# Router logits and gate scores with the weights as the loaded operand, in four column quarters of TensorE

## The chip, the cores and the metric

The kernel runs on one core of one Trainium2 chip. TensorE (PE in the profile; PEld is its weight load) multiplies, VectorE (DVE) does element-wise work and reductions, ScalarE (ACT) does copies and exponentials, GpSimd (POOL) does the rest of the element-wise work and issues the indexed transfers, and SyncE (SP) issues the ordinary transfers. The metric is the device time of one execution in microseconds (us), the median of several runs. Everything is float32; one float32 matmul of the program shows in the profile as two weight loads and two matmuls.

## The reference

Two decoder layers on x of 8 x 256 x 512 (2048 tokens of width 512). Two places matter here. The first is the feed-forward of layer 0, a mixture of 8 experts of which each token takes two:

```python
logits = h @ router_w.T                       # (2048, 512) @ (512, 8)
probs = jax.nn.softmax(logits, axis=-1)
vals, idx = lax.top_k(probs, 2)
```

The second is the feed-forward of layer 1, an attention in which each token picks one of 16 heads for its key and value:

```python
gating = jax.nn.softmax(x @ W_gate.T, axis=-1)   # (2048, 512) @ (512, 16)
idx = jnp.argmax(gating, axis=-1)
k_shared = one_hot(idx) . k ;  v_shared = one_hot(idx) * gating . v
```

Between and around them stand a differential attention, a long convolution, a causal self attention and a cross attention, each with a residual and a layer norm.

## The kernel before

Tokens come in 16 tiles of 128. The stages run one after another: `diff_attention`, `long_conv`, the expert blocks (`blocks`), `self_attention`, `cross_attention` and `routed_attention`.

**The router** (`router`, `route`, `token_tile`, `choose`, `send`, `table`). It runs in two halves of eight token tiles. The first half stands inside `long_conv` after head 15 of 32; there the order of instructions on each engine is made by the framework's scheduler when the program is built, so that convolution work (`ps_y` on TensorE, `z`, `yc`, `kv` on VectorE) stands between the router's. The second half stands in `blocks`, inside a section whose order on TensorE, VectorE and ScalarE is the order of the program text: blocks 0 to 2 of the experts (`gate_up`, and `turn`, which transposes the next block), with three or two token tiles after each, then `choose`. One `token_tile` transposes the tile to token-major form (`pt_c`, L731), copies it out by ScalarE (L737), takes mean and variance (L145, L146), norms the tile before it (L722), and computes the logits: four k-steps, each with 128 tokens as the loaded operand and 8 columns of router weights as the streamed one (`ps_r`, through `project`, L172), copied to `raw` by ScalarE (L744). `choose` turns `raw` into the two chosen experts by some thirty small VectorE operations; `send` computes each token's slot and scatters the rows by 16 indexed transfers on GpSimd (L789). The PSUM tag `tr` has two buffers, which `pt_c`, `ps_r` and `turn` share.

**The gates** (`gates` in `routed_attention`). The stage works in four groups of 512 tokens. `turned_group` transposes four token tiles (`pt`, L195) and ScalarE copies each of them into a quarter of `xT` (L196). `gates` then makes, for each of the four token tiles, four k-steps with 128 tokens loaded and 16 columns streamed (`ps_g`), and VectorE does the softmax and the maximum. `feature_block` (queries, `ps_f`), `token_block` (keys and values, `ps_t`), and `keys_turned` (`pt_k`) follow. A planner in `causal_attention` doses these pieces between the attention units: each piece has a cost (`MM` = 0.86, `TR` = 0.45 us, the gates 0.8), a slot by which it must be done, and a place in a queue; `fill` takes pieces from it up to a budget for each slot, `need` takes what is due. The order of the engines here is that of the program text too. The PSUM tag `mm` has three buffers. In attention units, `products` (L1264, L1274) uses TensorE in four column quarters: for each of four heads 32 loaded columns and up to 256 streamed ones, into 32 partitions of PSUM each.

`routed_weights` loads the weights of this stage before the cross attention begins.

Of the kernel before, what the change touches and what calls it, by code (L numbers as in the profile page):

```python
# [17 lines left out]
F32 = mybir.dt.float32  # L18
BF16 = mybir.dt.bfloat16
AF = mybir.ActivationFunctionType  # L20
ALU = mybir.AluOpType
# [29 lines left out]
def decoder_kernel(ctx: ExitStack, tc: tile.TileContext, a: dict, out: bass.AP):  # L51
# [117 lines left out]
    def project(ps, lhsT, rhs, n=KB):  # L169

        for k in range(n):
            nc.tensor.matmul(ps, lhsT=lhsT(k), rhs=rhs(k), start=(k == 0), stop=(k == n - 1))  # L172

    MM, TR = 0.86, 0.45

# [314 lines left out]
    def long_conv(router, load_experts, xh, ch, ps_t, meanwhile):  # L490
# [5 lines left out]
        with ExitStack() as st:  # L496
# [18 lines left out]
            for h in range(NH):  # L515
                i, at = divmod(h * NHEAD, P)
                hs = slice(at, at + NHEAD)
                xv, cv = xh[i], ch[i]
                wt = work.tile([P, D], F32, tag="wt", name="wt", bufs=3)
                nc.sync.dma_start(out=wt, in_=toeplitz(h))  # L520
                if h == 2:
                    load_experts()

                kv = work.tile([P, KB, B, NHEAD, NHEAD], F32, tag="kv", name="kv")
                for k in range(KB):
                    (nc.gpsimd if k == KB - 1 else nc.vector).tensor_tensor(  # L526
                        kv[:, k],
                        xv[:, k, :, hs].unsqueeze(2).broadcast_to(shape),
                        cv[:, k, :, hs].unsqueeze(3).broadcast_to(shape),
                        ALU.mult,  # L530
                    )
# [12 lines left out]
                nc.gpsimd.tensor_tensor(  # L544
                    r,
                    cv[:, :, :, hs],
                    us.unsqueeze(3).broadcast_to([P, KB, B, NHEAD]),
                    ALU.mult,
                )
                nc.gpsimd.tensor_tensor(r, r, xv[:, :, :, hs], ALU.add)  # L550
                yc = work.tile([P, KB, B, NHEAD], F32, tag="yc", name="yc")
                for lb in range(KB):
                    ps = psum.tile([P, B, NHEAD, NHEAD], F32, tag="y", name="ps_y")
                    project(
                        ps,
                        lambda k: wt[:, (lb - k) * P : (lb - k + 1) * P],
                        lambda k: kv[:, k],
                        n=lb + 1,
                    )
                    z = work.tile([P, B, NHEAD, NHEAD], F32, tag="z", name="z", bufs=3)  # L560
                    nc.vector.tensor_tensor(
                        z, ps, cv[:, lb, :, hs].unsqueeze(2).broadcast_to(shape), ALU.mult
                    )
                    nc.vector.tensor_reduce(yc[:, lb], z, AX.X, ALU.add)  # L564
                nc.gpsimd.tensor_tensor(xv[:, :, :, hs], r, yc, ALU.add)  # L565
                if h < 2:
                    for t in range(h * PH + 1, (h + 1) * PH, 2):
                        turn(t)
                    if h == 1:
                        x_first.close()  # L570
                if h == NH // 2 - 1:
                    tiles, choose, send, table = route(ps_t, xv, i)
                    for f in (*tiles, choose, send, table, meanwhile):
                        f()
            return route(ps_t, xh[1], 1)

# [42 lines left out]
    def experts(rt):  # L619
# [26 lines left out]
                    ].rearrange("e p c -> p e c"),  # L646
                )

        rw = rt.tile([P, KB, E], F32, tag="rw", name="rw")
        idx = index_row(rt, E, "idx_e")  # L650
        before = rt.tile([P, P], F32, tag="before", name="before")
        ones = rt.tile([P, P], F32, tag="ones_m", name="ones_m")
# [23 lines left out]
        def router(work, rows_late):  # L676
            nc.sync.dma_start(
                out=rw, in_=a["L0_ffn_router_w"].rearrange("(k p) e -> p k e", p=P)
            )

            nc.gpsimd.memset(ones, 1.0)
            nc.gpsimd.affine_select(
                out=before,
# [17 lines left out]
            def route(ps_t, xv, half):  # L701
# [22 lines left out]
                    )  # L724
                    nc.sync.dma_start(out=xd[tiles[i]], in_=r)

                def token_tile(i):
                    b = tiles[i] // 2
                    pt = ps_t.tile([P, KB, P], F32, tag="tr", name="pt_c")
                    for k in range(KB):  # L730
                        nc.tensor.transpose(pt[:, k, :], xv[:, k, b, :], ident)  # L731
# [7 lines left out]
                    rsqrt(rstd[:, i : i + 1], mv[:, i, 1:2], 1.0)  # L739
                    if i:  # L740
                        norm(i - 1)
                    pr = ps_t.tile([P, E], F32, tag="tr", name="ps_r")
                    project(pr, lambda k: xv[:, k, b, :], lambda k: rw[:, k, :])
                    nc.scalar.copy(raw[:, i, :], pr)  # L744

                def choose():
                    norm(PH - 1)

                    lg = rt.tile(shape, F32, tag="lg", name="lg", bufs=2)
# [61 lines left out]
                    for v in (v1, v2):  # L811
                        nc.vector.tensor_tensor(v, v, vs, ALU.mult)

                return [lambda i=i: token_tile(i) for i in range(PH)], choose, send, table

            return route

# [91 lines left out]
        def blocks(ps_t, buffers, late_tokens, meanwhile):  # L909


            with ExitStack() as st:
# [102 lines left out]
                with tc.manual_schedule(  # L1015
# [6 lines left out]
                    turn(0)  # L1022
                    for b in range(3):
                        if b:
                            tiles[3 * b - 1]()
                        gate_up(b)
                        load(b + 4)
                        for f in tiles[3 * b : 3 * b + 2]:
                            f()
                        turn(b + 1)  # L1030
                    choose()
                    gate_up(3)
# [643 lines left out]


    def routed_weights(w):
        return load_w(w, 0, a["L1_ffn_W_qkv"], 3 * D), load_w(
            w, 3 * D * KB, a["L1_ffn_W_gate"], H1  # L1680
        )

    def routed_attention(wqkv, wg):

# [2 lines left out]
        def prepare(work, pools, g, at, here):  # L1687
# [6 lines left out]
            ind = work.tile([P, TPG, H1], F32, tag="ind", name="ind")  # L1694
            itop = work.tile([P, TPG, H1], F32, tag="itop", name="itop")

            def gates():
                ps = pools.tile([P, TPG, H1], F32, tag="mm", name="ps_g")
                for ti in range(TPG):
                    project(  # L1700
                        ps[:, ti, :],
                        lambda k: xT[0][:, k, ti * P : (ti + 1) * P],
                        lambda k: wg[:, k, :],
                    )
                gate = work.tile([P, TPG, H1], F32, tag="gate", name="gate")
                nc.vector.tensor_copy(gate, ps)
                softmax_small(work, gate, H1)
                top = work.tile([P, TPG], F32, tag="top", name="top")
                first_max(work, gate, H1, idx, top, ind)
# [26 lines left out]
                nc.scalar.copy(kT, pt.rearrange("p t q -> p (t q)"))  # L1736

            xT, need = turned_group(work, pools, g)
            need.append((0, [(0.8, gates)]))
            need.append((0, feature_block(pools, qT, xT, wqkv, 0, 0, HD1**-0.5)))  # L1740
            for ti in range(TPG):
                need.append(
                    (0, token_block(pools, xT, wqkv, D, ti, lambda ps, ti=ti: key(ti, ps)))
                )
            for c in range(1, 3):
                need.append((0, feature_block(pools, qT, xT, wqkv, 0, c, HD1**-0.5)))
            need.append((0, [(TR, keys_turned)]))
            for c in range(3, KB):
                need.append((c, feature_block(pools, qT, xT, wqkv, 0, c, HD1**-0.5)))
# [146 lines left out]
```

## Time and profile before

| what | value |
|---|---|
| median of three runs | 2196.74 us (2194.0 to 2199.11) |
| the profiled execution, its time | 2205.52 us |
| its span from first to last instruction | 2203.7 us |
| TensorE busy | 2054.0 us, 93% of the span |
| VectorE busy | 1275.9 us, 58% |
| GpSimd busy | 826.9 us, 38% |
| ScalarE busy | 605.1 us, 27% |
| mean granted TensorE clock | 0.971 |

The profiled execution is a single one: its own time is 1.8 us over its span, and 8.8 us over the median of the timed runs. Durations in the rows below are of this execution. A timeline row gives the start in us, the duration, the engine, the line, the operation with output and inputs, the shapes and the count, and in brackets how long the engine was idle before and who ended that. The duration of a merged matmul row is from the first start to a modelled end; the distance to the next row's start is the time that TensorE spent on it.

### The profile page before, as it was taken

How to read it: one execution, taken by the hardware profiler on the slowest of the kernel's cores; microseconds unless marked ns; L12 is line 12 of the kernel's file. 1: busy time of each engine (PE TensorE's matmuls, PEld its weight loads, DVE VectorE, ACT ScalarE, POOL GpSimd, SP SyncE). 2: the span in 40 equal slices, each digit the busy share in tenths (PEclk: the TensorE clock that was granted, in tenths of full speed). 3: DMA queues.
4: the chain of work that ended last, by engine and by line, in shares of the span. 5: the costliest groups of instructions: out<-in, count | busy, mean ns of one | idle time of the engine just before them, and what ended most of it. 6: DMA issues, size and time to landing. Idle time of an engine off the chain costs nothing. (4 is left out here: it accounts for less than half of the span.)

```text
span 2203.7 us, 36445 instructions
## 1 busy us (share of the span) xinstructions
PE 2054.0 (93%) x15296; PEld 1264.8 (57%) x15296; DVE 1275.9 (58%) x1923; ACT 605.1 (27%) x773; POOL 826.9 (38%) x918
## 2 busy tenths in 40 slices
PE   8989999889999998999968999999999999999995
PEld 6646655544453464555545665656877875545543
DVE  4677777658888962222235756556344343576777
ACT  4545555410010021111113333330110110333342
POOL 2667777646557622000034544333000000142343
PEclk9989999989999999999979999999999999999998
DMA  6899802235133153131141201002100100000000
GB/s 220 331 384 381 311 1 69 78 93 186 34 115 120 29 172 121 60 144 63 43 144 30 77 20 58 2 1 96 36 22 20 39 0 1 1 11 11 11 18 32
DMA packets 110035, 197.61 MB, mean 90 GB/s; under 512 B 7088, under 2 KB 30768, under 8 KB 109872
## 3 DMA queue, kind: packets, MB, share of 16 engines
q1 hardware_dynamic: 104752, 178.49, 23.3%
q0 software_dynamic: 5120, 16.78, 2.2%
q8 instruction: 123, 2.02, 0.4%
q14 instruction: 40, 0.33, 0.0%
HBM read 93.54 MB, written 112.20 MB: 93 GB/s over the span
## 5 line engine op out<-in xcount | busy, mean ns | idle before, releaser
L1282 DVE RECIPROCAL rsum<-ps_pv 128x256 f32<-128x256 f32 x128 | 224.5, 1754 | 243.7 <-PE ps_pv L1274 243.4
L172 PE MATMUL ps_y<-kv,wt 128*128 128x512 f32 x640 | 281.1, 597 | 4.5 <-POOL kv L526 3.8
L1238 ACT ACTIVATE pT<-ps_k 128x1536 f32<-128x1536 f32 x128 | 185.8, 1451 | 286.0 <-PE ps_k L1230 282.1
L1178 DVE TENSOR_REDUCE neg<-rows 128x12 f32<-128x1536 f32 x128 | 223.0, 1742 | 54.1 <-POOL rows L1169 54.0
L1169 POOL TENSOR_SCALAR_AFFINE_SELECT rows<-rows 128x1024 f32<-128x1024 f32 x128 | 141.5, 1105 | 246.8 <-ACT rows L1167 246.5
L1167 ACT COPY rows<-ps_q 128x1536 f32<-128x1536 f32 x128 | 184.3, 1440 | 179.4 <-PE ps_q L1158 130.2
L1239 POOL TENSOR_SCALAR_AFFINE_SELECT pT<-pT 128x1024 f32<-128x1024 f32 x128 | 141.1, 1103 | 242.6 <-ACT pT L1238 242.4
L172 PEld LDWEIGHTS ps_y<-kv,wt 128*128 128x128 f32 x640 | 120.3, 191 | 153.6 <-issue 135.2
L1249 POOL TENSOR_TENSOR pT<-pT 128x512 f32<-128x512 f32 x112 | 145.7, 1301 | 9.3
L183 PE MATMUL ps_f<-xT,w_l1a 128*128 128x256 f32 x512 | 129.2, 400 | 12.2 <-ACT xT L196 12.2
L1084 POOL DMA_INDIRECT w_l1x<-ys,slots x32 | 32.7, 1023 | 279.8 <-DMA ys<-y_m 272.1
L183 PE MATMUL ps_t<-w_l1f,xT 128*128 128x512 f32 x256 | 121.9, 611 | 0.0
L183 PEld LDWEIGHTS ps_f<-xT,w_l1a 128*128 128x128 f32 x512 | 96.9, 197 | 33.8 <-ACT xT L196 14.3
L999 PE MATMUL po_m<-dn,hT 128*128 (+1 forms) x216 | 104.4, 621 | 12.0 <-ACT hT L992 10.5
L140 POOL TENSOR_SCALAR rstd<-bn_mv 128x1 f32<-128x1 f32 x80 | 16.6, 207 | 216.2 <-DVE bn_mv L146 208.1
L1274 PE MATMUL ps_pv<-pT,ones_v 128*32 128x256 f32 (+1 forms) x1152 | 84.7, 376 | 7.2 <-POOL pT L1249 7.0
L564 DVE TENSOR_REDUCE yc<-z 128x64 f32<-128x512 f32 x128 | 86.1, 674 | 6.2 <-POOL w_l1a L565 5.7
L981 DVE TENSOR_TENSOR h_b<-h_b,pg 128x352 f32<-128x352 f32 x36 | 18.8, 521 | 101.3 <-ACT h_b L980 101.3
L1158 PE MATMUL ps_q<-kz,qT 32*128 32x128 f32 x1536 | 62.2, 292 | 15.2 <-ACT pT L1238 13.3
L1158 PEld LDWEIGHTS ps_q<-kT,qT 32*128 32x128 f32 x1536 | 49.2, 188 | 44.4 <-issue 21.2
L1158 PEld LDWEIGHTS ps_q<-kz,qT 32*128 32x128 f32 x1536 | 49.8, 190 | 41.0 <-ACT pT L1238 26.2
L183 PE MATMUL ps_f<-xT,w_l 128*128 128x256 f32 x256 | 71.2, 406 | 0.9 <-POOL w_l L273 0.7
(326 smaller groups left out, 3768.7 us busy)
## 6 DMA issues: line engine op xcount, KB each, us to landing
xs<-zero SPq DMA_DIRECT2D x8, 4352.0 KB
ys<-zero SPq DMA_DIRECT2D x8, 4352.0 KB
filters<-in_L_xattn_k SPq DMA_DIRECT2D x4, 2560.0 KB
first_h<-xs SPq DMA_DIRECT2D x36, 256.0 KB
ys<-y_m SPq DMA_DIRECT2D x36, 256.0 KB
gu<-in_L_ffn_gate_up_proj SPq DMA_DIRECT2D x3, 2816.0 KB
wt<-filters SPq DMA_DIRECT2D x32, 256.0 KB
x<-in_x SPq DMA_DIRECT2D x16, 256.0 KB
```

The costliest lines, as they stand in the source:

```text
L172: nc.tensor.matmul(ps, lhsT=lhsT(k), rhs=rhs(k), start=(k == 0), stop=(k == n - 1))
L183: nc.tensor.matmul(ps[0], lhsT=lhsT(k), rhs=rhs(k), start=(k == 0), stop=(k == KB - 1))
L564: nc.vector.tensor_reduce(yc[:, lb], z, AX.X, ALU.add)
L999: nc.tensor.matmul(po, lhsT=hT[:m, i, :], rhs=dn[i][:m, bass.ds(e, 1), :], start=(i == 0), stop=(i == len(FCH) - 1),)
L1158: nc.tensor.matmul(block[:, s, j, :], lhsT=q(rows, c, b * S + i * P, P), rhs=k(rows, c, b * S + keys * P, P), start=True, stop=True,)
L1167: nc.scalar.copy(d.rearrange("p j s k -> p s j k"), block)
L1169: nc.gpsimd.affine_select(out=rows, in_=rows, compare_op=ALU.is_ge, fill=-FAR, base=0, pattern=[[0, 8], [-1, P]], channel_multiplier=1,)
L1178: return lambda: nc.vector.tensor_reduce(neg[u // upb % 2][:, :, :, c], d, AX.X, ALU.max, negate=True)
L1238: nc.scalar.activation(p[:, 0:3].rearrange("p j s q -> p s j q"), block, AF.Exp)
L1239: nc.gpsimd.affine_select(out=p[:, 0:2].rearrange("p j s q -> p (j s) q"), in_=p[:, 0:2].rearrange("p j s q -> p (j s) q"), compare_op=ALU ...
L1249: nc.gpsimd.tensor_tensor(p[:, 3], p[:, 1], p[:, 2], ALU.add)
L1282: nc.vector.reciprocal(r, ps[:, 1, :])
```

## The change

Two new helpers are used in both places. `columns_by_block` takes 512 tokens at once: each of the four k-steps has its weight columns as the loaded operand, 32 columns wide, in a column quarter of TensorE of its own, and the 512 tokens as the streamed one. The results stand in 32 partitions of one PSUM tile each, unsummed, and one ScalarE copy of 128 x 512 takes them out. `sum_of_blocks` then transposes the four 128 x 128 pieces of that copy and sums the four k-steps with one VectorE reduction. Since 32 columns are loaded where 8 or 16 are meant, the weight tiles get a zeroed tail (a GpSimd memset for the router, a VectorE memset for the gates), and the columns beyond are not read.

In the router, `token_tile` no longer computes logits: after the fourth and the eighth tile of a half, `columns_by_block` is called, and `logits` (the transposes and the sum) at the beginning of the next tile or of `choose`. In the routed attention, `gates` is split into `gate_parts` and `gates`, with a feature block between them, and the second feature block is moved ahead of the key blocks. The gate weights are loaded ahead of `W_qkv`.

```diff
+    def columns_by_block(ps, dst, w, n, rhs):
+        for k in range(KB):
+            nc.tensor.matmul(
+                ps[32 * k : 32 * k + 32, :],
+                lhsT=w[:, n * k : n * k + 32],
+                rhs=rhs(k),
+                start=True,
+                stop=True,
+            )
+        nc.scalar.copy(dst, ps)
+
+    def sum_of_blocks(dst, pt, parts):
+        for i in range(pt.shape[1]):
+            nc.tensor.transpose(pt[:, i, :], parts[:, i * P : (i + 1) * P], ident)
+        n = dst.shape[2]
+        nc.vector.tensor_reduce(
+            dst, pt.rearrange("p t (k r n) -> p t r n k", k=KB, n=n)[:, :, 0], AX.X, ALU.add
+        )
...
+            nc.gpsimd.memset(rows_w[:, KB * E :], 0.0)
...
+                def logits():
+                    pt = ps_t.tile([P, PH // 2, P], F32, tag="tr", name="pt_r")
+                    i, rows = part.pop()
+                    sum_of_blocks(raw[:, i : i + PH // 2, :], pt, rows)
+
-                def token_tile(i):
+                def token_tile(i, pool):
                     b = tiles[i] // 2
+                    if i == PH // 2:
+                        logits()
...
-                    pr = ps_t.tile([P, E], F32, tag="tr", name="ps_r")
-                    project(pr, lambda k: xv[:, k, b, :], lambda k: rw[:, k, :])
-                    nc.scalar.copy(raw[:, i, :], pr)
+                    if (i + 1) % (PH // 2) == 0:
+                        j = i + 1 - PH // 2
+                        rows = pool.tile([P, D], F32, tag="rpart", name="rpart", bufs=1)
+                        columns_by_block(
+                            ps_t.tile([P, D], F32, tag="tr", name="ps_r"),
+                            rows,
+                            rows_w,
+                            E,
+                            lambda k: xv[:, k, j : i + 1, :],
+                        )
+                        part.append((j, rows))
 
                 def choose():
+                    logits()
                     norm(PH - 1)
...
     def routed_weights(w):
-        return load_w(w, 0, a["L1_ffn_W_qkv"], 3 * D), load_w(
-            w, 3 * D * KB, a["L1_ffn_W_gate"], H1
-        )
+        g = 3 * D * KB
+        load_w(w, g, a["L1_ffn_W_gate"], H1)
+        nc.vector.memset(w[:, g + KB * H1 : g + KB * H1 + 32 - H1], 0.0)
+        return load_w(w, 0, a["L1_ffn_W_qkv"], 3 * D), w[:, g:]
...
+            def gate_parts():
+                columns_by_block(
+                    pools.tile([P, GT], F32, tag="mm", name="ps_g"), part, wg, H1, lambda k: xT[0][:, k, :]
+                )
+
             def gates():
-                ps = pools.tile([P, TPG, H1], F32, tag="mm", name="ps_g")
-                for ti in range(TPG):
-                    project(
-                        ps[:, ti, :],
-                        lambda k: xT[0][:, k, ti * P : (ti + 1) * P],
-                        lambda k: wg[:, k, :],
-                    )
+                pt = pools.tile([P, TPG, P], F32, tag="mm", name="pt_g")
                 gate = work.tile([P, TPG, H1], F32, tag="gate", name="gate")
-                nc.vector.tensor_copy(gate, ps)
+                sum_of_blocks(gate, pt, part)
...
-            need.append((0, [(0.8, gates)]))
+            need.append((0, [(MM, gate_parts)]))
             need.append((0, feature_block(pools, qT, xT, wqkv, 0, 0, HD1**-0.5)))
+            need.append((0, [(TR, gates)]))
+            need.append((0, feature_block(pools, qT, xT, wqkv, 0, 1, HD1**-0.5)))
             for ti in range(TPG):
...
-            for c in range(1, 3):
-                need.append((0, feature_block(pools, qT, xT, wqkv, 0, c, HD1**-0.5)))
+            need.append((0, feature_block(pools, qT, xT, wqkv, 0, 2, HD1**-0.5)))
```

More of the change, by code (lines that the diff above doesn't have):

```diff
@@ L572, in long_conv @@
                     tiles, choose, send, table = route(ps_t, xv, i)
-                    for f in (*tiles, choose, send, table, meanwhile):
+                    for f in tiles:
+                        f(work)
+                    for f in (choose, send, table, meanwhile):
                         f()
@@ L647, in load_gu_last @@
                 )
-        rw = rt.tile([P, KB, E], F32, tag="rw", name="rw")
+        rows_w = rt.tile([P, KB * E + 32 - E], F32, tag="rw", name="rw")
+        rw = rows_w[:, : KB * E].rearrange("p (k e) -> p k e", k=KB)
         idx = index_row(rt, E, "idx_e")
@@ L725, in norm @@
                     nc.sync.dma_start(out=xd[tiles[i]], in_=r)
-                def token_tile(i):
+                part = []
+                def logits():
[3 more added lines that the diff above has]
+                def token_tile(i, pool):
                     b = tiles[i] // 2
+                    if i == PH // 2:
+                        logits()
                     pt = ps_t.tile([P, KB, P], F32, tag="tr", name="pt_c")
@@ L812, in table @@
                         nc.vector.tensor_tensor(v, v, vs, ALU.mult)
-                return [lambda i=i: token_tile(i) for i in range(PH)], choose, send, table
+                return [lambda pool, i=i: token_tile(i, pool) for i in range(PH)], choose, send, table
             return route
@@ L1024, in blocks @@
                         if b:
-                            tiles[3 * b - 1]()
+                            tiles[3 * b - 1](work)
                         gate_up(b)
@@ L1028, in blocks @@
                         for f in tiles[3 * b : 3 * b + 2]:
-                            f()
+                            f(work)
                         turn(b + 1)
@@ L1695, in prepare @@
             itop = work.tile([P, TPG, H1], F32, tag="itop", name="itop")
-            def gates():
-                ps = pools.tile([P, TPG, H1], F32, tag="mm", name="ps_g")
-                for ti in range(TPG):
-                    project(
-                        ps[:, ti, :],
-                        lambda k: xT[0][:, k, ti * P : (ti + 1) * P],
-                        lambda k: wg[:, k, :],
-                    )
+            part = work.tile([P, GT], F32, tag="gpart", name="gpart", bufs=1)
+            def gate_parts():
+                columns_by_block(
+                    pools.tile([P, GT], F32, tag="mm", name="ps_g"), part, wg, H1, lambda k: xT[0][:, k, :]
+                )
+            def gates():
+                pt = pools.tile([P, TPG, P], F32, tag="mm", name="pt_g")
                 gate = work.tile([P, TPG, H1], F32, tag="gate", name="gate")
-                nc.vector.tensor_copy(gate, ps)
+                sum_of_blocks(gate, pt, part)
                 softmax_small(work, gate, H1)
```

## The prediction

> **What bounds the kernel now.** I read first the page's busy times (TensorE 93% of the span), then the two operations that go, by tile.
>
> ```profile
> PE 2054.0 (93%) x15296; PEld 1264.8 (57%) x15296; DVE 1275.9 (58%) x1923; ACT 605.1 (27%) x773; POOL 826.9 (38%) x918
> L172 PE MATMUL ps_r<-rw,first_h x64: 175/256/256, 632.0 to 648.1; 128*128 128x8 f32 x64
> L172 PE MATMUL ps_g<-w_l1f,xT x128: 262/263/374, 1847.1 to 2078.7; 128*128 128x16 f32 x128
> ```
>
> Eight or sixteen streamed columns take about as long as a weight load: these matmuls pay for loading tokens. The timeline shows a group's gates (third group), then the first half's token tiles:
>
> ```profile
> 1988.76 2.05 ACT L196 COPY xT<-pt 128x512 f32<-128x512 f32 x4
> 1989.39 0.66 PE L195 MATMUL pt<-ident,x 128*128 128x128 f32 x4 [0.65 <-ACT xT L196]
> 1989.89 3.74 PE L172 MATMUL ps_g<-w_l1f,xT 128*128 128x16 f32 x32
> 1993.48 3.01 PE L183 MATMUL ps_f<-xT,w_l1f 128*128 128x512 f32 x4
> ```
>
> ```profile
> 633.80 0.60 PE L731 MATMUL pt_c<-ident,first_h 128*128 128x128 f32 x4
> 634.24 0.96 PE L172 MATMUL ps_r<-rw,first_h 128*128 128x8 f32 x8
> 635.05 1.10 PE L172 MATMUL ps_y<-kv,wt 128*128 128x512 f32 x2
> ```
>
> From start to start: gates 3.59 us a group, logits 0.81 a tile (3.24 for four), four transposes 0.44, a 512-column float32 step 0.86. TensorE never pauses between them, and the chain of waits has the gates of three groups in it. In both places TensorE is the engine that ends things, with two exceptions, below.
>
> **Part 1: what one call costs.** The new product is eight matmuls (two per k-step) of 32 loaded and 512 streamed columns in four column quarters. The nearest rows have the same form, 128 rows by 32 columns, float32:
>
> ```profile
> 1948.83 0.86 PE L1264 MATMUL ps_pv<-pT,v_r 128*32 128x256 f32 x16
> 1949.51 0.61 PE L1274 MATMUL ps_pv<-pT,ones_v 128*32 128x256 f32 x8
> 1950.05 0.71 PE L1221 MATMUL ps_k<-qT,kT 32*128 32x256 f32 x8
> ```
>
> L1274 is four quarters of two matmuls, 256 columns each: 0.54 us. One quarter alone would be half of 0.86, so 0.43: the four run side by side, with 0.11 for starting and changing form. At 512 columns: 0.86 + 0.11 = 0.97 us. The Trainium skill speaks against this ("TensorE: Matmul & The Clock Gate", Part 3, The mechanism): a weight load overlaps running matmuls only when its row group differs, and here all four have all rows. By that rule the call is serial, 4 x 0.86 = 3.44 us, and the change gains nothing. L1264 and L1274 have all rows too, and serial they would be 2.6 and 1.7 us, not 0.68 and 0.54. I take the row, 0.97 (bounds 0.9 and 3.44). Transposes: 0.44. So 1.41 us of TensorE per 512 tokens.
>
> Around it: a ScalarE copy of 128x512 (0.59, as L737), with some 0.2 us of signalling on either side; a VectorE reduction of 128 or 256 elements a row, estimated at 0.3 and 0.55 from L1723's 1.07 for 512, against the removed gate copy's 0.22 (and 16 ScalarE copies of 0.17 on `raw`).
>
> **Part 2: the gates, four groups.** Removed 3.59, added 1.41. But there is a new wait. The old gates began with token tile 0 while ScalarE still copied tile 3; the new product streams all four tiles in its first k-step. The transposes end at 1989.89, the fourth copy (four in 2.05 us from 1988.76) at 1990.81: TensorE waits about 0.95 us. Everything on its queue waits with it, as no other engine is behind TensorE there; bounds 0.6 and 1.1. The transposes of the parts stand a feature block (3.4 us) later, which hides the copy; if that cover went, 0.9 a group. The softmax chain on VectorE (3.3 us) is then hidden by the moved second feature block. VectorE's extra 0.33 is covered: it is busy 63.2 of 86 us in the window from 1975. Net for groups 1 to 3: 3.59 - 1.41 - 0.95 = 1.2 us each, 3.7 in all.
>
> Group 0 is different, as windows with the granted clock (the number after the POOL column) show:
>
> ```profile
> 1847.00:1850.50 3.50, 3.50 (x20) 3.43 (x19) 0.00 (x0) 1.06 (x3) 0.00 (x0) 0.57 0.01 2
> 1850.50:1854.00 3.50, 3.50 (x17) 3.50 (x18) 0.10 (x1) 0.00 (x0) 0.00 (x0) 0.50 0.00 0
> 1854.00:1857.00 3.00, 3.00 (x4) 1.19 (x4) 2.33 (x12) 0.26 (x1) 0.00 (x0) 0.50 0.00 0
> 1857.00:1859.20 2.20, 2.20 (x5) 0.91 (x4) 0.20 (x1) 0.00 (x0) 0.00 (x0) 0.84 0.00 0
> ```
>
> The clock stays at half through 6.56 us of gates and comes back only about 4.1 us into the feature block, at 1857.8. Gates and feature block take 12.07 us (1847.14 to 1859.21). The same page (Part 1: The HAM clock gate) says about 3.4 us of sustained activity release the clock; the row says 16-column matmuls do not count. The new product streams 512 columns at once: 0.95 wait, then 0.97 + 3.44 of work with half of 4.1 us lost (2.05), and 0.44 of transposes: 7.85 us, a gain of 4.2. By that 3.4 us it would be 4.6; if the clock comes back at 1857.8 whatever is done, only about 1.4. I take 4.2.
>
> Gates together: 3.7 + 4.2 = 7.9; less a tenth for slots that end on another engine, 7 us.
>
> **Part 3: the router's first half.** TensorE loses 8 x 0.81 = 6.5 us and gains 2 x 1.41 = 2.8: 3.7 less. The waits for copies are filled by convolution matmuls, as now. But VectorE loses nothing here, and after the tiles it becomes the bound:
>
> ```profile
> 660.00:680.00 20.00, 19.59 (x49) 8.20 (x48) 20.00 (x63) 0.00 (x0) 10.05 (x12) 1.00 0.21 71
> 697.07 1.99 PE L172 MATMUL ps_y<-kv,wt 128*128 128x512 f32 x2 [3.75 <-POOL kv L526]
> ```
>
> From 660 to 680 it is busy without a gap, and until 694.7 GpSimd issues the 16 scatters, for which TensorE then waits 3.75 us. What is gained before counts only as far as the slots (673) are ready earlier. During the tiles VectorE works about 2.05 of each 2.19 us, and its idle gaps add up to some 5 us. I take 2.5 us, between 0 and 4; the scheduler's new order could also lose a us.
>
> **Part 4: the second half.** Here the order is the text's. After block 0 two token tiles, `turn` and a third tile now run without logits: ScalarE's copies (0.59 each) become the limit, and of 3 x 0.88 us I find 2.0 gained (the next `gate_up` waits for `xT`). After block 1 the product is followed directly by its own transposes: TensorE waits for the copy, about 0.95 us, and both `tr` buffers are held. Worked through copy by copy: from the fourth tile to `gate_up` 5.0 us against 4.9. After block 2, 4.05 against 4.0. So 2 us, between 0 and 3. `choose`, behind these on VectorE, starts no later: the norm before it still ends last.
>
> **Part 5: small things.** Sixteen columns of memset on VectorE before the cross attention stand where the chain is on VectorE: 0.1 us, 0 to 0.3 (the tile is free, its readers ended before the last norm). The router's GpSimd memset is far from the chain. The order of two weight loads on SP, 340 us ahead of use, costs nothing; no transfer is added, and the scatters and `xd` stores keep their place.
>
> **Sum.** 7 + 2.5 + 2 - 0.1 = 11.4 us from the profiled 2205.5: 2194.1. Against the median of the timed runs, 2196.7: 2185.3. The profiled run lies 8.8 us above that median; one place may be why. TensorE stands still for 10.5 us (below), until the last scatter of the second half has landed, with no operand missing that the trace shows.
>
> ```profile
> 849.09 5.36 PE L999 MATMUL po_m<-dn,hT 128*128 x6 [10.47 <-ACT hT L992]
> ```
>
> **Rivals.** (a) Only the gates pay: VectorE and the scatters eat the first half, and ScalarE's copies the second. For it: the full VectorE row and the two `tr` buffers. Then 2196.7 - 7 = 2190. (b) The quarters run one after another, as the page says: 3.44 + 0.44 per call. Gates: 1.2 us longer in groups 1 to 3 (3.88 + 0.95 against 3.59), 1.7 shorter in group 0; first half 1.3 and second half 3 longer. Sum +6: 2203, slower. It decides once a call takes more than about 2.7 us. Against it: L1264, with its own streams per quarter. (c) The 10.5 us halt changes: ScalarE and VectorE reach it some instructions earlier or later. If it is in the timed runs and goes, 2175; if a second one arises in the first dispatch, 2196 to 2203. Nothing in the trace tells. (d) The planner and the scheduler place other pieces so that nothing is gained: 2196; for it, that the gates' planned cost rises from 0.8 to 1.31 while the true one falls.
>
> **How the numbers follow.** Forecast 0.58 (2185, its own range 2180 to 2190); (a) 0.18, (b) 0.08, (c) 0.10 shared between its ends, (d) 0.06. A difference of 0.2%, 4.4 us, is about what a measurement of this kernel can tell from none. Faster: the forecast, (a) and half of (c), less a little for overlaps: 0.78. Same: (d) and edges, 0.09. Slower: (b) and half of (c), 0.13. The range 2176 to 2197 holds forecast, (a), (d) and most of the fast end of (c).
>
> **What would show it.** Right: `ps_g` has eight matmuls of 128*32 per group, 0.97 us to the next row, after a TensorE wait of nearly 1 us for `xT`; the half-clock stretch in group 0 ends near 1852 (less what was gained before); `ps_r` two calls per half; VectorE still full after the first half's tiles. Wrong: a `ps_g` of over 2.7 us, an idle row on `gate_parts` well over 1 us, or a later start of the first scatter.

## The result, and the profile after

| | before | after |
|---|---|---|
| median of 14 runs each | 2194.25 us (2186.92 to 2203.61) | 2178.59 us (2167.78 to 2185.04) |
| ratio of after to before | | 0.9931, 95% interval 0.9915 to 0.9947 |
| the profiled execution: time, span | 2205.52, 2203.7 us | 2181.91, 2180.2 us |
| mean granted TensorE clock in it | 0.971 | 0.974 |

The change makes the kernel 15.7 us faster, 0.69%; 11.4 us were predicted. The median lies 1.4 us below the range that the prediction gave its forecast (2180 to 2190) and inside the whole range (2176 to 2197); the runs of before were 2.5 us faster than the median from which the forecast was counted. In a second series of runs the ratio was 0.993 (0.9906 to 0.9953), 13.8 us. The two profiled executions differ by 23.5 us; some ten of those do not belong to the change (the halt, at the end).

The page's busy times, then the two new products by tile and the reductions that sum them:

```profile
PE 2035.0 (93%) x15136; PEld 1238.0 (57%) x15136; DVE 1276.5 (59%) x1928; ACT 606.8 (28%) x765; POOL 827.2 (38%) x919
```

```profile
L178 PE MATMUL ps_r<-first_h,rw x16: 592/604/617, 636.7 to 643.6; 128*32 128x512 f32 x16
L192 DVE TENSOR_REDUCE raw<-pt_r x4: 281/286/292, 640.4 to 812.9; 128x32 f32<-128x128 f32 x4
L178 PE MATMUL ps_g<-xT,w_l1f x32: 592/617/1062, 1831.9 to 2053.8; 128*32 128x512 f32 x32
L192 DVE TENSOR_REDUCE gate<-pt_g x4: 391/408/425, 1838.6 to 2062.6; 128x64 f32<-128x256 f32 x4
```

TensorE is 19.0 us less busy, with the same 93%. A single new matmul shows 0.6 us, yet eight of them don't take 4.8: their records overlap. What a call costs is seen in TensorE's timeline of after, from a row's start to the next row's. First a router call in the first half, then the gates of the second group:

```profile
636.68 1.06 PE L178 MATMUL ps_r<-first_h,rw 128*32 128x512 f32 x8
637.67 1.12 PE L172 MATMUL ps_y<-kv,wt 128*128 128x512 f32 x2
...
1891.11 0.66 PE L217 MATMUL pt<-ident,x 128*128 128x128 f32 x4 [0.56 <-ACT xT L218]
1892.58 1.06 PE L178 MATMUL ps_g<-xT,w_l1f 128*32 128x512 f32 x8 [0.81 <-ACT xT L218]
1893.58 3.70 PE L205 MATMUL ps_f<-xT,w_l1f 128*128 128x512 f32 x8
1897.21 0.95 PE L1202 MATMUL ps_q<-kT,qT 32*128 32x128 f32 x24
1898.09 0.66 PE L190 MATMUL pt_g<-ident,gpart 128*128 128x128 f32 x4
1898.58 3.60 PE L205 MATMUL ps_f<-xT,w_l1f 128*128 128x512 f32 x8
```

A call takes 0.99 us in the router and 1.00 in the gates, where 3.24 and 3.59 us of matmuls stood before; the transposes of its result take 0.49. Ahead of the gates is the new wait, 0.81 us for ScalarE's copy of the fourth token tile. There is none ahead of the transposes: a feature block and a piece of the attention stand between. The sum of a group is 0.81 + 1.00 + 0.49 = 2.30 us against 3.59, so 1.29 gained. The windows of the whole second group, between the first token transposes of two groups, agree; the granted clock (after the POOL column) is 1.00 in both. Before, then after:

```profile
1908.22:1987.22 79.00, 77.33 (x755) 40.92 (x749) 54.32 (x76) 28.73 (x28) 29.32 (x28) 1.00 0.02 8
```

```profile
1889.02:1966.81 77.79, 75.31 (x735) 37.90 (x729) 53.69 (x76) 29.32 (x29) 29.36 (x28) 1.00 0.02 8
```

79.00 to 77.79: 1.21 us. The stages, from rows of TensorE's timeline (the convolution from the first `ps_y` to the blocks' first transposes, the blocks from there to `ps_pl` of `send`, the routed stage from its first token transposes to the end):

| stage | before, and again | after, and again | predicted gain |
|---|---|---|---|
| convolution with the router's first half | 299.4, 301.2 us | 297.9, 297.9 us | 2.5 |
| blocks 0 to 2 with its second half | 38.02, 38.01 us | 35.25, 35.25 us | 2.0 |
| routed stage | 360.2, 360.2 us | 352.9, 350.2 us | 7 |

Gains: 1.5 to 3.3, 2.8, and 7.3 to 10.1 us.

One more reading is needed for the runs below. In every series the time follows the mean granted clock: the 14 runs of after reach from 2167.78 us at 0.982 to 2185.04 at 0.973, and a straight line through a series falls 1.2 to 1.9 us for each thousandth of clock. Two single profiles can differ by several us in a stage that nobody touched: the second half, unchanged in the kernel with the gates alone, lasted 39.6 us in its profile and 38.0 in those of before, with a clock of 0.89 in the window from 815 to 830. So the runs are judged by their ratios, and stages by rows whose clock is shown. Kernels named together ran together, beside the same runs of before.

### The profile page after: what moved, and what is told of

It reads as the page before. It is cut to its first block, busy times and chain, and to the rows that moved or that the text cites. A ratio compares the mean times of both kernels' runs of the same rounds, so it can differ in the third digit from the quotient of the medians.

```text
span 2180.2 us, 36118 instructions
## 1 busy us (share of the span) xinstructions
PE 2035.0 (93%) x15136; PEld 1238.0 (57%) x15136; DVE 1276.5 (59%) x1928; ACT 606.8 (28%) x765; POOL 827.2 (38%) x919
## 5 line engine op out<-in xcount | busy, mean ns | idle before, releaser
L205 PEld LDWEIGHTS ps_t<-w_l1f,xT 128*128 128x128 f32 x256 | 45.6, 191 | 47.0 <-issue 44.2
```

Of the source, the lines that this page charges most:

```text
L205: nc.tensor.matmul(ps[0], lhsT=lhsT(k), rhs=rhs(k), start=(k == 0), stop=(k == KB - 1))
```

## The experiments

**First series: each half of the change alone, the quarters taken away, and before again.** Theory: the quarters work side by side and both places gain. Rival: the gain comes from elsewhere, or from only one of the two.

Gates only, the router as before:

```diff
-                    if (i + 1) % (PH // 2) == 0:
-                        ...
-                        columns_by_block(...)
+                    pr = ps_t.tile([P, E], F32, tag="tr", name="ps_r")
+                    project(pr, lambda k: xv[:, k, b, :], lambda k: rw[:, k, :])
+                    nc.scalar.copy(raw[:, i, :], pr)
```

> Theory 1 (each place pays for itself): the gates' part alone gains 7 us as predicted, 7.3 as the two profiles' last stage shows; 2187 against 2194, ratio 0.9967. Theory 2 (the stretch between TensorE's halt of 10.5 us at 838 us and the change is what was gained): under 3 us from the gates. On the halt itself: ScalarE and VectorE execute the same number of instructions before it as in the kernel before. If it hangs on the place in the instruction stream, it is in this profile again, about 10 us long, just as the second half's scatters end; if it is a chance of the one execution, it is absent here.

Router only, the gates as before:

```diff
-            need.append((0, [(MM, gate_parts)]))
+            need.append((0, [(0.8, gates)]))
             need.append((0, feature_block(pools, qT, xT, wqkv, 0, 0, HD1**-0.5)))
-            need.append((0, [(TR, gates)]))
-            need.append((0, feature_block(pools, qT, xT, wqkv, 0, 1, HD1**-0.5)))
```

> Theory 1: the router's part alone gains 4 to 5 us (1.5 in the convolution, 2.75 in the expert blocks), ratio 0.998. Theory 2: if the halt is in every execution of the kernel before and in none of the changed router, it gains about 15 us here, ratio 0.993, and the gates nothing in comparison. In the profile no halt by either theory of place; by chance it may show.

One quarter, the whole change with the four k-steps summed in the first 32 columns:

```diff
-                ps[32 * k : 32 * k + 32, :],
+                ps[:32, :],
...
-                start=True,
-                stop=True,
+                start=(k == 0),
+                stop=(k == KB - 1),
```

> The change without the four quarters: the same eight matmuls of 32 loaded and 512 streamed columns, but all k-steps accumulate in the first quarter, so that they must run one after another; 32 partitions are copied and turned, and no sum over blocks is left. If the gain comes from the quarters running side by side, a call takes 8 x 0.43 = 3.44 us instead of 1.0, the gates of groups 1 to 3 take 0.9 us longer than before the change, and the kernel is at 2194 to 2200 (ratio 1.000 to 1.003), with a slight gain in group 0 by the clock. If the swap of operands alone is what pays, it is as fast as the change, 2179.

Before again:

> The kernel before once more, for its profile. Halt by place: TensorE again idle for about 10 us before the L999 matmul near 849 us. Halt by chance: no such row, and a span nearer to 2192.

| kernel | median | ratio to before (2207.14 us, 46 runs), 95% |
|---|---|---|
| gates only | 2199.2 us (17 runs) | 0.9959 (0.994 to 0.9977) |
| router only | 2202.59 us (22 runs) | 0.9969 (0.9954 to 0.9984) |
| one quarter | 2209.48 us (14 runs) | 1.0008 (0.9987 to 1.0029) |
| before again | 2205.49 us (one run) | |

The gates are worth 9.0 us of 2207, the router 6.8. The product of the two ratios is 0.9928, the whole change has 0.9931: the parts add. Router only gives the blocks their whole gain (35.24 us). Its routed stage, whose code is that of before, lasted 363.7 us in the profile where before has 360.2, and the difference is in the second group. In TensorE's timeline its gates take 5.40 us to the next row, where before takes 3.59 (start 1910.81, next row 1914.40); the windows from 1907 on show the clock falling in the middle of them:

```profile
1906.74 5.57 PE L172 MATMUL ps_g<-w_l1f,xT 128*128 128x16 f32 x32
1912.14 5.18 PE L205 MATMUL ps_f<-xT,w_l1f 128*128 128x512 f32 x8
```

```profile
1907.00:1910.50 3.50, 3.50 (x25) 3.50 (x24) 0.00 (x0) 0.66 (x2) 1.22 (x1) 0.69 0.01 2
1910.50:1914.00 3.50, 3.50 (x12) 2.47 (x12) 1.20 (x6) 0.26 (x1) 0.00 (x0) 0.50 0.00 0
```

The last kernel of the third series, which has the old gates too, shows the same: 82.31 us for the second group in both, 79.00 in the two profiles of before. In all nine profiles with the new gates in quarters this group lasts 77.3 to 77.8 us. So with the old gates a second loss of clock, worth 3.3 us, was there in two executions of four; how often the timed runs had it is not known.

One quarter has the same swapped operands, the same streams of 512 tokens and smaller transposes, and gains nothing. TensorE's timeline of that kernel, again the gates of the second group:

```profile
1914.70 3.62 PE L178 MATMUL ps_g<-xT,w_l1f 128*32 128x512 f32 x8 [0.81 <-ACT xT L218]
1918.25 3.70 PE L205 MATMUL ps_f<-xT,w_l1f 128*128 128x512 f32 x8
```

3.55 us from row to row against 1.00: the same eight matmuls run 3.6 times as fast in four quarters. So the gain is in the quarters and not in the swap; rival (b) of the prediction is this kernel. Its call of 3.55 us is beyond the 2.7 us at which the sign was said to turn; the time is 2 us above before, with an interval from -3 to +6, and rival (b) had said +6.

**Second series: what the first half waits for, and the two new waits.** The prediction took VectorE for the bound of the first half after the tiles. If it is, work taken off VectorE there must shorten the stage.

After again:

> The changed kernel once more. Theory 1, the change is worth its own work and the 10.5 us halt of TensorE at 838 to 849 us comes or stays away by chance: the ratio to before lies at 0.991 to 0.996, and the profile may show the halt or not; with it, the blocks run later by 10 us than in the first profile of this kernel. Theory 2, the change itself takes the halt away: it is absent again, and the ratio lies at 0.988 to 0.993. In both, the first half's stage from the first ps_y to the blocks' first transposes lasts 296.5 to 298 us where the granted clock stays at 1.00 between 675 and 715 us, and 2 to 3 us more where it falls to 0.8 to 0.9 there.

Norm on ScalarE, for the first half's eight tiles:

```diff
+                    if half == 0:
+                        m = work.tile([P, 1], F32, tag="shift", name="shift", bufs=PH)
+                        nc.gpsimd.tensor_scalar(
+                            m, mv[:, i, 0:1], rstd[:, i : i + 1], -1.0, ALU.mult, ALU.mult
+                        )
+                        nc.scalar.activation(r, r, AF.Identity, bias=m, scale=rstd[:, i : i + 1])
```

> The changed kernel with the first half's eight normalizations of 128x512 (0.55 us each on VectorE) given to ScalarE, which stands idle from 645 to 700 us; GpSimd makes one more 128x1 operand for each. Theory 1, in the first half VectorE is the bound once the router's tiles leave TensorE (busy 15.0 of 15 us from 660 to 675 us), so that only about 1.3 of the 3.7 us of TensorE work came back: with 4.4 us less on VectorE the first scatter starts 2.5 to 4 us earlier than in the changed kernel (673.5 us there), the stage lasts 1.5 to 3 us less, and the time is 0.999 to 0.998 of the changed kernel's. Theory 2, TensorE and its granted clock decide, VectorE only follows: first scatter within 1 us, stage within 0.5 us at equal clock.

No wait, the stream of the gates cut and the second half's first transposes one tile later:

```diff
-                    if i == PH // 2:
+                    if i == PH // 2 + half:
                         logits()
...
+                    lambda k, a, z: xT[0][:, k, a:z], ((0, 3 * P), (3 * P, 4 * P)),
```

> The changed kernel with its two visible waits taken away: the gates' stream is cut at token 384, so that the first three token tiles are multiplied while ScalarE copies the fourth (four more matmuls and weight loads of 32 columns in each group), and the second half's first turned products come one tile later, behind other work. Theory 1, the waits of 0.81 us ahead of ps_g and of 0.71 us ahead of pt_r are on the path: the wait for xT shrinks to 0.0 to 0.3 us, the cut stream takes 0.75 + 0.25 us, the routed stage loses 0.4 to 0.6 us in each of four groups (352.9 to about 351 us), the blocks up to the send 0.5 to 0.7 us; the time 0.998 to 0.9995 of the changed kernel's. Theory 2, the time comes back as the next wait (ScalarE's copy or GpSimd's chains end as late as before): routed stage within 0.5 us.

Both edits:

> Both of the two edits before on the changed kernel: normalizations of the first half on ScalarE, the gates' stream cut at token 384, the second half's first products turned one tile later. If both theories 1 hold, the gains add: stage of the first half 1.5 to 3 us shorter, routed stage 2 us, blocks 0.6 us: 4 to 5.5 us below the changed kernel (a ratio to before of 0.989 to 0.992 where the changed kernel has 0.992 to 0.994). If theories 2 hold, within 1 us of it.

| kernel | median of 6 | ratio to before (2193.99 us, 11 runs), 95% |
|---|---|---|
| after again | 2180.24 us | 0.993 (0.9906 to 0.9953) |
| norm on ScalarE | 2181.72 us | 0.9934 (0.991 to 0.9957) |
| no wait | 2173.78 us | 0.9901 (0.9877 to 0.9926) |
| both | 2179.6 us | 0.9921 (0.9896 to 0.9946) |

*Norm on ScalarE* did not come out as either theory said. VectorE was busy 9.92 of 15 us between 645 and 660 where it had been 14.20, yet the first scatter started 186.8 us after the first `ps_y` instead of 185.5, and the stage lasted 304.0 us instead of 297.9. Its timelines of TensorE and of VectorE show where the time went:

```profile
649.64 0.66 PE L190 MATMUL pt_r<-ident,rpart 128*128 128x128 f32 x4 [2.48 <-ACT rpart L185]
...
703.40 26.87 PE L172 MATMUL ps_y<-kv,wt 128*128 128x512 f32 x56 [3.04 <-DVE kv L548]
```

```profile
698.85 0.42 DVE L564 TENSOR_REDUCE us<-u 128x32 f32<-128x256 f32 x1 [10.28 <-POOL r L566]
```

The copies of `rpart` now stand behind norms in ScalarE's queue (2.48 us), and VectorE, with less to do, stands still for 10.28 us at the end of the scatters: it waits for GpSimd. Then TensorE waits 3.04 us for VectorE, with half of its clock granted (0.50 in the window from 700 to 705).

So VectorE's work is not what ends the stage behind the scatters. The stretch ahead of them, from the last logits in `raw` to the first scatter, is another matter, and this kernel does not decide on it. VectorE's rows of the last `raw`, in after and then here, and the windows from 660 to 675, likewise:

```profile
647.95 0.28 DVE L192 TENSOR_REDUCE raw<-pt_r 128x32 f32<-128x128 f32 x1
650.33 0.29 DVE L192 TENSOR_REDUCE raw<-pt_r 128x32 f32<-128x128 f32 x1 [1.71 <-PE pt_r L190]
```

```profile
660.00:675.00 15.00, 13.59 (x36) 5.97 (x35) 15.00 (x48) 0.00 (x0) 7.12 (x8) 1.00 0.06 18
660.00:675.00 15.00, 14.17 (x38) 6.38 (x37) 14.93 (x48) 0.00 (x0) 8.63 (x12) 1.00 0.13 36
```

Seven of the eight norms had stood ahead of that `raw`, and the edit made `raw` itself 2.5 us later. From there to the first scatter VectorE is as full as it was, and the stretch took 24.1 us in place of 25.3. No run took VectorE work out of this stretch alone, so whether it is the bound there is not shown.

*No wait* did what it was meant to do where it was made. In TensorE's timeline the second group's wait is down to 0.32 us, and the second half's first transposes stand behind a token tile and a `turn`:

```profile
793.09 1.06 PE L178 MATMUL ps_r<-w_l1a,rw 128*32 128x512 f32 x8
794.09 0.66 PE L766 MATMUL pt_c<-ident,w_l1a 128*128 128x128 f32 x4
794.86 0.66 PE L217 MATMUL pt<-ident,first_h 128*128 128x128 f32 x4
795.42 0.66 PE L190 MATMUL pt_r<-ident,rpart 128*128 128x128 f32 x4
...
1881.39 1.07 PE L178 MATMUL ps_g<-xT,w_l1f 128*32 128x384 f32 x16 [0.32 <-ACT xT L218]
```

Blocks 34.73 us (35.25 in after), second group 77.31 us (77.79): 0.52 and 0.48, as expected, and the third group gained 0.48 too. The routed stage as a whole did not follow: it lasts 350.1 us in this profile and in that of after again, since the first group was 1.0 us longer, at a clock of 0.94 against 0.97, and the last as long as before. So theory 1 holds for the waits, and their sum over the stage is not shown. The medians differ by 6.5 us, and the two intervals overlap; the rest is not explained by the edits. This profile begins the convolution 5 us earlier than that of after again, in a part that no edit touches. *Both* lies between the two.

**Third series: the queue behind the scatters.** If VectorE waits for GpSimd, then what GpSimd owes after its sixteen scatters is the bound. In after, TensorE, VectorE and GpSimd read there:

```profile
697.43 32.86 PE L172 MATMUL ps_y<-kv,wt 128*128 128x512 f32 x72 [2.71 <-POOL kv L548]
```

```profile
695.81 1.28 DVE L586 TENSOR_REDUCE yc<-z 128x64 f32<-128x512 f32 x2 [5.23 <-POOL w_l1a L587]
```

```profile
673.50 1.26 POOL L833 DMA_INDIRECT xs<-xn,slots  x1 [0.19 <-DVE slots L829]
...
694.07 0.96 POOL L833 DMA_INDIRECT xs<-xn,slots  x1 [0.30 <-issue]
695.05 0.73 POOL L587 TENSOR_TENSOR w_l1a<-r,yc 128x256 f32<-128x256 f32 x1
695.73 0.63 POOL L566 TENSOR_TENSOR r<-w_l1a,us 128x256 f32<-128x256 f32 x1
696.31 1.06 POOL L548 TENSOR_TENSOR kv<-w_l1a 128x512 f32<-128x512 f32 x1
```

Two things of GpSimd's stand behind the scatters: the `kv` for which TensorE waits, and ahead of it the addition of `yc` (L587), which frees a buffer for which VectorE waits. The third series moves only the `kv` of the two heads:

```diff
-                    (nc.gpsimd if k == KB - 1 else nc.vector).tensor_tensor(
+                    (nc.gpsimd if k == KB - 1 and h - NH // 2 not in (5, 6) else nc.vector).tensor_tensor(
```

on the changed kernel,

> The changed kernel with two products of the long convolution (the fourth kv of heads 21 and 22, 128x512) given to VectorE; in the changed kernel GpSimd makes them after its sixteen scatters (673.5 to 695 us), and TensorE waits 2.71 us for the first of them at 697 us and is then granted 0.86 and 0.80 of its clock for 10 us. Theory 1, GpSimd's queue behind the scatters ends the first half's stage, so that TensorE work taken out ahead of it comes back only as far as the first scatter starts earlier: the wait goes (0 to 1 us stays), the granted clock stays at 0.95 to 1.00 between 695 and 710 us, and the stage from the first ps_y to the blocks' first transposes falls from 297.9 to 294 to 296 us; time 2 to 4 us below the changed kernel. Theory 2, VectorE (19.8 of 25 us busy from 675 to 700 us) can't take 1.4 us more: the wait turns into one for VectorE's kv of the same length, stage 297.5 to 299 us, time within 1 us.

on the kernel without the two waits,

> The same two products on VectorE, together with the gates' stream cut at token 384 and the second half's first products turned one tile later. Theory 1: the gains add, 2 to 4 us for the stage of the first half, 0.5 us in the blocks and 0.5 us in each group of the routed stage: 4 to 7 us below the changed kernel, a ratio to before of 0.989 to 0.991 where the changed kernel has 0.992 to 0.993. Theory 2 (the products on VectorE bring nothing): 2 to 3 us below the changed kernel.

and on the kernel before:

> The kernel before with the same two products on VectorE, nothing else changed. In the kernel before TensorE waits 3.75 us for GpSimd's kv at 697 us. Theory 1, GpSimd's queue behind the scatters is the bound of the first half there too: the wait goes, the stage (299.4 us and 301.2 us in the two profiles of before) falls to 296 to 298 us, the time by 2 to 4 us. Theory 2, VectorE full: no change. The 10.5 us halt of TensorE in the blocks, if it belongs to the program as laid out and not to a chip, may come or go here, since the instruction streams are shifted by two.

| kernel | median | ratio to before (2206.32 us, 32 runs), 95% | convolution |
|---|---|---|---|
| after, kv on VectorE | 2193.12 us (11 runs) | 0.9941 (0.9922 to 0.996) | 300.8 us |
| the same, no wait | 2188.68 us (6 runs) | 0.9927 (0.9901 to 0.9954) | 300.1 us |
| before, kv on VectorE | 2211.22 us (22 runs) | 1.0018 (1.0001 to 1.0035) | 302.0 us |

Theory 1 fell in all three; the kernel before was even 0.2% slower with the edit. Theory 2 came nearer, but the stage grew beyond what it said (300.8 us, at most 299 expected), and its reason is wrong: VectorE is not too full there, it stands still. Its timeline in the first of these, then TensorE's:

```profile
696.25 1.28 DVE L586 TENSOR_REDUCE yc<-z 128x64 f32<-128x512 f32 x2 [4.63 <-POOL w_l1a L587]
697.45 2.88 DVE L548 TENSOR_TENSOR kv<-w_l1a 128x512 f32<-128x512 f32 x1
```

```profile
700.39 3.78 PE L172 MATMUL ps_y<-kv,wt 128*128 128x512 f32 x4 [4.38 <-DVE kv L548]
```

The `kv` was moved behind the same wait: it starts at 697.45, once GpSimd has freed `yc`, and takes 2.88 us beside GpSimd's work on the tokens, where one alone takes 0.68 (see the end). TensorE's wait grew from 2.71 to 4.38 us.

**Fourth: free the buffer too.**

```diff
-                yc = work.tile([P, KB, B, NHEAD], F32, tag="yc", name="yc")
+                yc = work.tile([P, KB, B, NHEAD], F32, tag="yc", name="yc", bufs=4)
```

> The kernel with the cut stream, the later products and the two kv on VectorE, and now four buffers in place of two for yc, the sums that GpSimd adds into the tokens. In the two profiles with kv on VectorE alone, VectorE itself stands 4.6 us until GpSimd, back from its sixteen scatters, has added yc at 695.5 us and so frees the buffer, and only then makes the kv for which TensorE waits 4.38 us. Theory 1, this one addition behind the scatters is what ends the first half's stage: with two more buffers VectorE's wait goes, TensorE's wait shrinks from 4.4 to 0 to 1.5 us, the granted clock stays above 0.9 between 695 and 710 us, the stage from the first ps_y to the blocks' first transposes lasts 294 to 297 us (300.1 without the buffers, 297.9 in the changed kernel); time 3 to 6 us below the kernel without them. Theory 2, other operands of GpSimd's (the u of the next head) are as late: VectorE waits as long on the next instruction, stage 299 to 301 us.

2174.66 us (6 runs) beside 2194.25 (11 runs): ratio 0.9901 (0.9863 to 0.994). In the profile theory 1 holds. The order of the instructions on VectorE and GpSimd is the same as without the buffers, VectorE's wait of 4.6 us for `yc` is gone (one of 1.96 us for the next head's `u` is left), and the convolution lasts 295.9 us instead of 300.1. TensorE's timeline, and the windows with the clock, first here and then in after:

```profile
675.74 26.02 PE L172 MATMUL ps_y<-kv,wt 128*128 128x512 f32 x60 [0.86 <-DVE kv L548]
702.20 1.98 PE L172 MATMUL ps_y<-kv,wt 128*128 128x512 f32 x4 [0.44 <-DVE kv L548]
705.95 34.60 PE L172 MATMUL ps_y<-kv,wt 128*128 128x512 f32 x80 [1.77 <-DVE kv L548]
```

```profile
695.00:700.00 5.00, 5.00 (x13) 2.21 (x12) 3.04 (x5) 0.00 (x0) 5.00 (x10) 1.00 0.66 199
700.00:705.00 5.00, 3.74 (x9) 1.13 (x7) 5.00 (x4) 0.00 (x0) 5.00 (x7) 1.00 0.37 117
695.00:700.00 5.00, 2.57 (x5) 1.07 (x6) 4.19 (x6) 0.00 (x0) 4.98 (x9) 0.86 0.47 131
700.00:705.00 5.00, 5.00 (x11) 2.26 (x10) 1.31 (x3) 0.00 (x0) 5.00 (x7) 0.80 0.60 191
```

The clock stays at 1.00 through the place where it was 0.86 and 0.80 in after. From the first scatter on, TensorE's waits sum to 3.1 us, to 6.0 without the buffers and to 3.6 in after. So against the changed kernel itself, whose stage lasts 297.9 us (296.9 in *router only*, with the same order there), the waits shrank by only 0.5 us, and most of what was gained goes with the clock (0.14 and 0.20 of 5 us each are 1.7 us, an estimate).

In time less is shown than in the profile. The ratio without the buffers was 0.9927, and its interval overlaps this one. The kernel without the two waits alone has 0.9901 as well, against 0.993 for the change, and six runs each do not separate these. The deeper buffer was not tried without the moved `kv`.

## Why the prediction came out right, point by point

**One call (0.97 us).** Right: 0.99 to 1.00, transposes 0.44 to 0.49. The rule weighed against it, from the Trainium skill's page "TensorE: Matmul & The Clock Gate", would have made it 3.44; the kernel with one quarter measured what serial means, 3.55. The same page has a line that would have spoken for the change, in "Why this matters for your kernels": products with few loaded columns go side by side in quarters of their own, 2.38 times as fast for three. Here four ran 3.6 times as fast.

**The wait for `xT` (0.95 us) and groups 1 to 3 (1.2 us each).** Right: 0.81, and 1.21 in the group whose clock was full in both profiles. The other two moved by 2.4 and 0.7 us between the first profiles, with the clock going from 0.96 to 0.98 in the one and from 0.92 to 0.91 in the other.

**Group 0 (4.2 us).** About right, and less certain than the prediction had it. The whole group fell from 64.75 to 61.75 us in the first profile of after and to 60.27 in the second: 3.0 and 4.5 us. The difference is the clock. The windows over the gates and the start of the feature block, in the first profile and then in the second:

```profile
1832.00:1835.00 3.00, 3.00 (x10) 0.82 (x11) 0.00 (x0) 0.59 (x1) 0.00 (x0) 0.50 0.02 5
1835.00:1838.00 3.00, 3.00 (x8) 1.22 (x8) 0.00 (x0) 0.00 (x0) 0.00 (x0) 0.97 0.00 0
```

```profile
1826.00:1829.50 3.50, 2.69 (x13) 1.02 (x13) 0.00 (x0) 1.42 (x3) 0.00 (x0) 1.00 0.02 5
1829.50:1833.00 3.50, 3.50 (x12) 1.72 (x11) 0.87 (x3) 0.60 (x1) 0.00 (x0) 1.00 0.00 0
```

In the first, half of the clock was granted from the product on and nearly all of it some 3.2 us later, as argued (near 4.1 was taken); in the second it never fell. The gates together, predicted at 7 us, measured 9.0 alone (interval 5 to 13). The prediction gave a gain by the clock to the first group only; the second group with the old gates can lose clock too (3.3 us in two profiles of four).

**The router's first half (2.5 us).** The size was right (1.5 to 3.3 between the profiles), the reason was half right. "What is gained before counts only as far as the slots are ready earlier" held: the last logits stood in `raw` 162.0 us after the first `ps_y` in the profiles of before and 160.2 in those of after, and the first scatter started after 187.2 and 187.7 and after 185.5 us, 1.7 to 2.3 earlier. "After the tiles VectorE becomes the bound" fits as far as the slots: VectorE is full there, and the stretch from `raw` to the first scatter has 25.1 to 25.7 us in all four profiles; that VectorE sets its length was argued, not shown. Behind the slots it fails: VectorE stands still 5.23 us for GpSimd (5.75 in before). Between the slots and TensorE's next work stand the sixteen scatters, the addition of `yc` and the `kv`; of these the wait for the addition is the one that a run took away. Behind it lies a stretch of lowered clock, with which the stage varies by one to two us from execution to execution.

An earlier scatter is not always a shorter stage. In *one quarter* and in *both*, for which the scheduler made another order of the convolution, it started 1.4 and 0.4 us earlier than in after, and the stage was 3.0 and 4.0 us longer. The prediction had allowed a us for such a new order.

**The second half (2.0 us).** Mis-sized: 2.8. The part after block 0 gained 2.2, as worked out. For blocks 1 and 2 the copy-by-copy working gave 5.0 against 4.9 and 4.05 against 4.0 us, a small loss; measured were 4.73 against 4.90 and 3.62 against 3.99, a small gain. The wait for ScalarE's copy ahead of the transposes was taken at 0.95 us; in TensorE's timeline of after it is 0.71 in one place and 0.18 in the other, where a `turn` of the next block fills it:

```profile
801.82 0.66 PE L190 MATMUL pt_r<-ident,rpart 128*128 128x128 f32 x4 [0.71 <-ACT rpart L185]
...
812.19 0.66 PE L190 MATMUL pt_r<-ident,rpart 128*128 128x128 f32 x4 [0.18 <-ACT rpart L185]
```

**VectorE's reductions** were estimated at 0.3 and 0.55 us and took 0.29 and 0.41.

**The rivals.** (a) is refuted by the router alone, (d) by each of the two parts. (b) is refuted by the quarters. (c), that the halt of 10.5 us goes away, seemed to be what the first two profiles show; the series show that it does not belong to the change, as told below. Without it the two profiles differ by 13 us, near the timed difference.

## What to carry to other kernels

Matmuls that load 128 tokens to stream 16 columns keep the weight loads busy all the time (3.50 of 3.50 us in the window from 1907 above). With the weights loaded into four column quarters and 512 tokens streamed, four products cost 0.99 us, where one quarter took 3.55 for them; without the quarters the swap was worth nothing here. Before calling an engine with full slices the bound of a whole stage, follow it to its next idle row and ask what it waits for there: VectorE was full up to the slots, and then stood still for one buffer that GpSimd could free only after a queue of scatters. Moving work between engines moved that wait here; a deeper buffer removed it, in the one profile that there is.

## What was not expected of the hardware

**The halt belongs to the series, not to the kernel.** In the blocks, at the end of the second half's sixteen scatters, TensorE stood still for 10.5 us in the first profile of before and not in that of after. TensorE's timeline of the router-only kernel has it, that of after again has not, though the kernel's text up to there is the same:

```profile
846.38 4.73 PE L1043 MATMUL po_m<-dn,hT 128*128 x6 [10.61 <-ACT hT L1036]
```

```profile
841.74 0.60 PE L217 MATMUL pt<-ident,first_h 128*128 128x128 f32 x4
842.42 2.84 PE L1043 MATMUL po_m<-dn,hT 128*128 x6
```

All four kernels of the first series show it, all three of the third, none of the four of the second, nor the last one. The runs of before agree: at a mean granted clock of 0.973 they take 2200.07 to 2203.59 us in the first series and 2200.25 to 2205.93 in the third, but 2195.84 in the second and 2191.91 and 2194.25 beside the last. Third series and last run were on the same chip. What sets it when a program is put on the chip remains open. ScalarE and VectorE stand still until about 3.3 us after the start of the last scatter (845.28 and 848.54 us in before), near the time at which it lands (2.7 us from issue to landing in after), with no operand missing that the trace shows. Comparisons within a series are free of it; the two single profiles of before and after were not.

**VectorE beside GpSimd.** A `kv` of 0.68 us took 2.88 us, and in the same kernel 3.57 at 700.86, where GpSimd worked on the same tokens at the same time. The traces of before, of after, of the first kernel of the third series and of the last one hold 388 `kv` on VectorE. The 59 that ran beside no element-wise operation of GpSimd's on two operands all took 0.66 to 0.69 us, the 28 among them beside its issuing of scatters too; the 329 beside such operations took 0.67 to 3.60, and 288 of these more than 0.70. The Trainium skill's page "SBUF — State Buffer" (SBUF: two separate sides) says that the two engines share one port pair, which one operation holds to its end, and that a VectorE operation with two inputs in SBUF meets it when GpSimd's reads SBUF. `kv` has two such inputs, and the lengths fit; the lock itself no trace shows.
